# Chunk-wise start and half-wise end of layer 1, with its score rows and two own-row loads moved, in a four-layer graph network

## The chip, the cores and the metric

The kernel runs on one core of a Trainium2 chip. The metric is the device time of one execution in microseconds. Below, PE is the tensor engine (PEld its weight loads), DVE the vector engine, ACT the scalar engine, POOL the GpSimd engine and SP the sync engine, which here only issues transfers.

## The reference

Four graph layers on 2708 nodes with 512 features; after each, the input is added and the rows are normalised. The adjacency matrix `adj` is 2708 x 2708 with about four entries per row besides the diagonal. What matters here is layer 1:

```python
type_sum_a = adj_a @ x
type_sum_b = adj_b @ x
attn_a = sigmoid(concatenate([type_sum_a, x], axis=1) @ Wa.T + ba)
attn_b = sigmoid(concatenate([type_sum_b, x], axis=1) @ Wb.T + bb)
h = x @ W_sa
s_left = h @ a_sa[0, :Hd]
s_right = h @ a_sa[0, Hd:]
scores = s_left[:, None] + s_right[None, :]
e = where(adj_a != 0, exp(-leaky_relu(scores, 0.01)), 0.0)
attn = e / (sum(e, axis=1, keepdims=True) + 1e-05)
x_a = attn @ h
x_b = adj_b @ (x @ W_gcnb) + b_gcnb
return sigmoid(attn_a * x_a + attn_b * x_b)
```

`adj_a` and `adj_b` are both `adj`. Layer 0 is `x - (adj @ x) * (diag + 1)` times a weight plus a bias, layer 2 a normalised neighbour sum, layer 3 a graph convolution with tanh.

## The kernel before, in words

The kernel finds the nonzero entries of `adj` in layer 0 and then works on lists of edges. Rows are taken in NB = 24 blocks of R = 113 rows. The edges of a block, some 450, stand in a list of 512 places, that is EC = 4 chunks of 128. To sum a block's neighbours, POOL gathers the source rows of the four chunks from a table in HBM (`gather`, L602: four indirect DMAs, one per chunk, with one row of the table per partition; places without an edge are skipped), and PE multiplies each chunk by a 128 x 113 matrix that holds each edge's value in the column of its target row. [...]

The order of work is written out by hand (`manual_schedule`), so each engine executes its instructions in the order of the program, and waits in that order.

Layer 0 leaves `table[0]` in HBM, one row of 1029 float32 per node: a one, `h`, `x @ W_gcnb`, then the node's `s_right` and gate terms. It leaves the node's `s_left` in a column of `xr`. The last store to the table is that of window 21 (`store0(KB - 1)`, L1297), and the gathers of layer 1 wait for it. Behind that store, SP loads own rows.

Own rows are a block's own 113 rows of `table[0]`, needed for the diagonal. They lie in NO = 9 places inside buffers that layer 0 has done with (`own_place`, L643). Blocks 0 to 3 are loaded by SP at L1278, 4 to 6 at L1295, 7 and 8 at L1299 (`load_own1`; each is two DMAs, of 112 rows and of 1). From block 9 on, POOL gathers them with one indirect DMA each (`gather_own1`, L1394), in step i for block i + 8, once the place is free.

Layer 1 itself (from L1634): `s_left` is needed as a row on all partitions. `spread_left(i)` (L1377) has PE transpose four blocks' columns into PSUM and DVE copy them out (L1383). Six such calls stand before the loop. The loop has one step per block i:

- `gather1(i + 2)`: POOL's four issues into one of three buffers `gath`, after PE has done with the block that used it.
- `sums1(i)`: PE sums the rows weighted with the edge values, `l1s`, L1441, 8 matmuls in 16 passes.
- `both1(i - 1)`: DVE joins the two sums of the block before: `rec`, `l1a` (L1492), `l1v` (L1497), then ACT's tanh.
- `values1(i + 2)`: ACT makes the value matrices `s`, in two parts.
- `scored_sums1(i)`: PE sums with the scores, `l1e`, L1451, 16 passes. Its PSUM tile exists once, so it waits for `l1a` of block i - 1.
- `scores1(i + 1)`: DVE adds and applies the leaky slope (L1424, L1428; the tile `e`), ACT the exponential; `mask1` (L1434) clears places without an edge.
- `stats1(i - 1)`, `gates1(i)`, `gated1(i)` (`l1b`, L1471 and L1475), then `mask1(i + 1)`, `scale1`, `norm1(i - 2)` with its store to `table[1]`, and `source_sum(i)`.

After the loop come `both1(23)`, `stats1(23)` and `norm1(23)`, the last store to `table[1]`, and then the gathers of layer 2, which wait for it. Before the loop DVE also works out `in_block` and `block_of` (L1338, L1344), used by `source_sum`, and `plus` (L1590). `keep_warm` and `keep_busy` are matmuls into tiles that nobody reads.

Of the kernel before, what the change touches and what calls it, by code (L numbers as in the profile page):

```python
# [18 lines left out]
R = 113  # L19
# [428 lines left out]
def sparse_stack(  # L448
# [148 lines left out]
    def over_chunks(row):  # L597
        return row[:, None, :].to_broadcast([P, EC, R])
# [63 lines left out]
    with ExitStack() as phase:  # L662
# [632 lines left out]
                    load_own1(i)  # L1295
        keep_busy(4)
        store0(KB - 1)  # L1297
        for i in range(7, NO):
            load_own1(i)  # L1299


    gpool = ctx.enter_context(tc.tile_pool(name="gpool", bufs=1))
# [26 lines left out]
    for k, t in enumerate((ba_bc, bb_bc)):  # L1329
# [4 lines left out]
    nc.vector.reciprocal(inverse, inverse)  # L1334


    in_block = gpool.tile([P, NB, NS], I32, name="in_block")
    nc.vector.tensor_scalar(  # L1338
        in_block, where_all, 1.0 / R, 0.5 / R - 0.5, op0=ALU.mult, op1=ALU.add
    )  # L1340
    block_of = gpool.tile([P, NB, NS], FP, name="block_of")
    for g, (c0, _) in enumerate(SEGS):
        at = slice(8 * g, 8 * g + 8)
        nc.vector.tensor_scalar(  # L1344
            block_of[:, :, at], in_block[:, :, at], float(c0), None, op0=ALU.add
        )
    deg_k = gpool.tile([P, KB], FP, name="deg_k")

    def source_sum(b):
# [14 lines left out]
    def halves(t, r):  # L1364
        return t[:r, :].rearrange("p (k d) -> p k d", k=2)
# [11 lines left out]
    def spread_left(i, n=4):  # L1377
        ps = ps_sp.tile([P, n, P], FP, tag="sp", name=f"sl{i}")
        for k in range(n):
            nc.tensor.transpose(  # L1380
                ps[:, k, :R], cols[:R, i + k, 0:1].to_broadcast([R, P]), ident[:R, :R]
            )
        nc.vector.tensor_copy(s_left[:, i : i + n, :], ps[:, :, :R])  # L1383
# [21 lines left out]
    def gather1(i):  # L1405
        gather(gath[i % NGB], i, table[0], W1)

    def values1(i, chunks):

        if i not in edge_s:  # L1410
            edge_s[i] = spool.tile([P, EC, R], FP, tag="s", name=f"s1_{i}", bufs=3)
            nc.scalar.copy(gath[i % NGB][:, :, W1], inverse[:, i, :])
        for c in chunks:
            t = spool.tile([P, R], FP, tag="away", name=f"away1_{i}_{c}")
            nc.scalar.activation(t, iota_r, AF.Abs, bias=nrow[:, i, c : c + 1])
            nc.scalar.activation(  # L1416
                edge_s[i][:, c, :], t, AF.Relu,
                bias=edges[:, i, c, 1:2], scale=nvalue[:, i, c : c + 1],
            )

    def scores1(i):

        e = spool.tile([P, EC, R], FP, tag="e", name=f"e{i}")
        nc.vector.tensor_tensor(  # L1424
            e, gath[i % NGB][:, :, SR : SR + 1].to_broadcast([P, EC, R]),
            over_chunks(s_left[:, i, :]), ALU.add,
        )
        nc.vector.scalar_tensor_tensor(e, e, 0.01, e, op0=ALU.mult, op1=ALU.max)  # L1428
        nc.scalar.activation(e, e, AF.Exp, scale=-1.0)
        edge_e[i] = e  # L1430

    def mask1(i):
        e = edge_e[i]
        nc.vector.scalar_tensor_tensor(e, edge_s[i], 0.0, e, op0=ALU.is_gt, op1=ALU.mult)  # L1434

    def sums1(i):
        g, s, r = gath[i % NGB], edge_s.pop(i), rows(i)
        sum_s[i] = ps_1s.tile([P, 2, D], FP, tag="s1", name=f"l1s{i}")
        for k, at in enumerate(s_at):
            for c in range(EC):  # L1440
                nc.tensor.matmul(  # L1441
                    sum_s[i][:r, k, : at.stop - at.start], lhsT=s[:, c, :r], rhs=g[:, c, at],
                    start=(c == 0), stop=(c == EC - 1),
                )

    def scored_sums1(i):
        g, e, r = gath[i % NGB], edge_e.pop(i), rows(i)
        sum_e[i] = ps_1e.tile([P, 2, D], FP, tag="e1", name=f"l1e{i}")
        for k, at in enumerate(e_at):
            for c in range(EC):  # L1450
                nc.tensor.matmul(  # L1451
                    sum_e[i][:r, k, k : k + at.stop - at.start], lhsT=e[:, c, :r],
                    rhs=g[:, c, at], start=(c == 0), stop=(c == EC - 1),
                )

    def gates1(i):

# [21 lines left out]
        )  # L1479
        nc.scalar.activation(vb[:r, :], vb[:r, :], AF.Copy, scale=gate[:r, 1:2])  # L1480

    def both1(i):

        r, agg = rows(i), sum_e.pop(i)
        rec = small.tile([P, 1], FP, tag="rec", name=f"rec{i}")
        nc.vector.scalar_tensor_tensor(
            rec[:r, :], agg[:r, 0, 0:1], 1e-5, ediag[:r, i : i + 1], op0=ALU.add, op1=ALU.add
        )
        nc.vector.reciprocal(rec[:r, :], rec[:r, :])
        nc.vector.tensor_mul(rec[:r, :], rec[:r, :], gate1.pop(i)[:r, 0:1])  # L1490
        va = work.tile([P, D], FP, tag="u", name=f"l1a{i}")
        nc.vector.scalar_tensor_tensor(  # L1492
            halves(va, r), halves(own1.pop(i)[:, 1 : D + 1], r), ediag[:r, i : i + 1],
            agg[:r, :, 1 : H + 1], op0=ALU.mult, op1=ALU.add,
        )
        v = work.tile([P, D], FP, tag="v", name=f"l1v{i}")
        nc.vector.scalar_tensor_tensor(  # L1497
            v[:r, :], va[:r, :], rec[:r, :], vb1.pop(i)[:r, :], op0=ALU.mult, op1=ALU.add
        )

        nc.scalar.activation(v[:r, :], v[:r, :], AF.Tanh, scale=0.5)
        v1[i] = v

    def stats1(i):
        r, v = rows(i), v1[i]
        nc.vector.scalar_tensor_tensor(
            v[:r, :], v[:r, :], 0.5, xr[:r, i, :], op0=ALU.mult, op1=ALU.add
        )
        stats = small.tile([P, 6], FP, tag="stats", name=f"st_l1_{i}")
        nc.vector.bn_stats(stats[:r, :], v[:r, :])  # L1510
        k = i % 2
        if k == 0 or i >= NB - 2:
            mv2[0] = small.tile([P, 2, 4], FP, tag="mv4", name=f"mv_l1_{i}")
        mv = mv2[0]
        nc.vector.bn_aggr(mv[:r, k, 0:2], stats[:r, :])
        v1[i] = v, mv[:, k, :]
        if k == 0 and i < NB - 2:
            return

        at = slice(k, k + 1) if i >= NB - 2 else slice(0, 2)  # L1520
        n = at.stop - at.start
        nc.vector.tensor_scalar(mv[:r, at, 1], mv[:r, at, 1], 1e-5, None, op0=ALU.add)
        nc.gpsimd.tensor_tensor(
            mv[:r, at, 2], mv[:r, at, 1], root[:r, :].to_broadcast([r, n]), ALU.pow
        )
        unscaled[0] = r, mv, at
# [60 lines left out]

    plus = const.tile([P, NB], FP, name="plus")
    inv_norm = const.tile([P, NB], FP, name="inv_norm")
    nc.vector.tensor_scalar(plus, adiag, 0.0, None, op0=ALU.is_gt)  # L1590

    def row_norms(at, on_pool=True):
        n = at.stop - at.start
# [40 lines left out]
    gather1(0)  # L1634
    values1(0, range(EC))
    gather1(1)
    values1(1, range(EC))
    for i in range(0, NB, 4):
        spread_left(i)
    spread_bias(bg_bc)  # L1640
    scores1(0)
    mask1(0)
    for i in range(NB):
        if i + 2 < NB:
            gather1(i + 2)
# [24 lines left out]
        if i > 1:  # L1670
            norm1(i - 2)
        if i + 1 == NB:
            norm1(i - 1)
        if i + 1 == NB:
            nc.sync.dma_start(out=b3_bc[0:1, :], in_=b3[None, :])
            nc.sync.dma_start(out=w3_sb, in_=w3T.rearrange("(b p) o -> p b o", p=P))
        if i < KB:
            source_sum(i)
        if i == KB:
            source_sums_out()  # L1680
            row_norms(slice(0, KB))
    copy_norm(0)
    copy_norm(1)
    keep_warm(ps_sp, "sp", [P, 4, P], 8)
    both1(NB - 1)
    spread_row(b3_bc, "b3")
    stats1(NB - 1)
    scale1()
    norm1(NB - 1)
    deg_ps = source_sums_in()  # L1690
# [234 lines left out]
```

## Time and profile before

| | us |
|---|---|
| time, median of 3 runs | 973.66 |
| lowest and highest run | 972.88, 977.18 |
| the profiled execution's own time | 958.69 |
| its span | 956.9 |
| PE / DVE / ACT / POOL busy in it | 884.8 / 685.3 / 526.3 / 465.5 |

Layer 1's first gather is issued at 414.26 us of the span, its loop runs to about 607, and layer 2's first gather is issued at 618.51. The profiled execution is one execution; stretches of it are compared with stretches of it, and a difference found so is carried over to the median. Matmul records show a modelled end, so PE's busy time says less than its waits. Rows of POOL's indirect DMAs show the time of issuing, not of the transfer.

### The profile page before, as it was taken

What the parts mean: (1) busy time and instruction counts of PE and PEld (TensorE: products, weight loads), DVE (VectorE), ACT (ScalarE), POOL (GpSimd) and SP (SyncE); (2) the same over time, 40 slices, a digit from 0 to 9 for tenths busy, and PEclk for the clock granted to TensorE, in tenths of its full rate; (3) what the DMA queues carried; (4) which work ended last, traced back from release to release, by engine and by line L of the source; (5) the groups of instructions that cost most, each with busy time, mean ns of one, the idle gap of its engine ahead of it and who ended that gap; (6) DMA issues with size and microseconds to landing.
All of it is one profiled execution on the core that took longest, in us unless ns stands there. A gap on an engine that the chain in (4) does not pass through costs nothing.

```text
span 956.9 us, 11163 instructions
## 1 busy us (share of the span) xinstructions
PE 884.8 (92%) x2957; PEld 489.4 (51%) x2957; DVE 685.3 (72%) x1811; ACT 526.3 (55%) x1221; POOL 465.5 (49%) x518
## 2 busy tenths in 40 slices
PE   6889999999999999989999999798888899999993
PEld 2446565556565565557777777433233334444441
DVE  7788798888888853148999999777777436565553
ACT  5776676867677672347777777344544312222221
POOL 3323131432323230057777753377777477766630
PEclk7879999999999999989999999989999999999997
DMA  9986887988878454388999976367777466555531
GB/s 245 323 208 184 216 229 207 272 223 220 227 206 238 152 166 126 115 286 292 349 330 342 341 276 236 95 188 213 212 218 217 131 170 189 163 174 162 151 107 32
DMA packets 133717, 201.73 MB, mean 211 GB/s; under 512 B 82658, under 2 KB 82704, under 8 KB 133647
## 3 DMA queue, kind: packets, MB, share of 16 engines
q0 software_dynamic: 39024, 118.69, 40.2%
q1 hardware_dynamic: 94623, 82.25, 30.2%
q8 instruction: 26, 0.43, 0.2%
q14 instruction: 44, 0.36, 0.1%
HBM read 182.81 MB, written 27.80 MB: 220 GB/s over the span
## 4 chain that ended last, share of the span: by engine, by line
PE 58%; DMA 14%; DVE 14%; issue 5%; ACT 4%; SPq 3%; POOL 2%; POOLq 0%; DVEq 0%; ACTq 0%
PE o_l L588 15%; DMA gath<-table,source 11%; PE l3a L617 8%; PE hb L588 7%; PE h L588 7%; PE l0a L617 6%; PE l2a L617 2%; PE fetched L929 2%; POOL gath L604 2%; PE unread L1585 2%; DVE l1b L1471 1%; SPq L691 1%; DMA gath<-in_x_dram 1%; DVE l1b L1475 1%; DVE l1a L1492 1%
## 5 line engine op out<-in xcount | busy, mean ns | idle before, releaser
L604 POOL DMA_INDIRECT gath<-table,source x288 | 305.0, 1059 | 102.7 <-issue 49.0
L604 POOL DMA_INDIRECT gath<-in_x_dram,source x96 | 97.4, 1015 | 224.9 <-issue 190.7
L617 PE MATMUL l2a<-gath,s_left 128*113 128x512 f32 (+1 forms) x192 | 97.2, 624 | 17.6 <-DMA gath<-table,source 17.4
L1451 PE MATMUL l1e<-gath,e 128*113 128x257 f32 (+3 forms) x384 | 88.4, 383 | 10.4 <-DVE l1a L1492 10.4
L617 PE MATMUL l3a<-gath,s 128*113 128x512 f32 (+1 forms) x192 | 88.3, 603 | 2.7 <-DMA gath<-table,source 2.7
L1441 PE MATMUL l1s<-gath,s 128*113 128x256 f32 (+3 forms) x384 | 89.8, 387 | 0.0
L617 PE MATMUL l0a<-gath,s 128*113 128x512 f32 (+1 forms) x192 | 87.5, 596 | 0.1
L588 PE MATMUL o_l<-shared,xi_own 128*113 128x512 f32 (+1 forms) x192 | 86.5, 593 | 0.8 <-ACT xi_own L581 0.7
L588 PE MATMUL hb<-w_gc_sb,xi_own 128*128 128x512 f32 (+1 forms) x176 | 83.3, 601 | 0.0
L1451 PEld LDWEIGHTS l1e<-gath,e 128*113 128x113 f32 (+1 forms) x384 | 66.2, 177 | 32.7 <-PE l1s L1441 19.4
L588 PE MATMUL o_l<-w_sb,uw_own 128*128 128x512 f32 (+1 forms) x176 | 82.7, 614 | 0.2
L588 PE MATMUL h<-w_sa_sb,xi_own 128*128 128x259 f32 (+1 forms) x352 | 80.8, 382 | 0.0
L1441 PEld LDWEIGHTS l1s<-gath,s 128*113 128x113 f32 (+1 forms) x384 | 69.2, 181 | 17.8 <-ACT s L1416 1.5
L588 PEld LDWEIGHTS h<-w_sa_sb,xi_own 128*128 128x128 f32 (+1 forms) x352 | 64.8, 185 | 19.8 <-issue 6.1
L617 PEld LDWEIGHTS l2a<-gath,s_left 128*113 128x113 f32 (+1 forms) x192 | 30.4, 181 | 73.9 <-DMA gath<-table,source 53.9
L1844 ACT ACTIVATE y<-l3v,mv_l 113x512 f32<-113x512 f32 (+1 forms) x24 | 19.5, 813 | 86.2 <-DVE mv_l L1840 79.2
L588 PEld LDWEIGHTS o_l<-shared,xi_own 128*113 128x113 f32 (+1 forms) x192 | 33.9, 177 | 49.2 <-issue 47.1
L617 PEld LDWEIGHTS l0a<-gath,s 128*113 128x113 f32 (+1 forms) x192 | 33.5, 179 | 40.7 <-issue 35.5
L617 PEld LDWEIGHTS l3a<-gath,s 128*113 128x113 f32 (+1 forms) x192 | 32.5, 180 | 41.2 <-issue 37.9
L1818 DVE SCALAR_TENSOR_TENSOR l3v<-o_l,d_inv,b_bc 113x512 f32<-113x512 f32 (+1 forms) x25 | 18.1, 728 | 48.1 <-PE o_l L588 48.1
L1308 DVE TENSOR_SCALAR s<-niota_r,nrow,edges 128x113 f32<-128x113 f32 x192 | 51.5, 344 | 0.0
L876 DVE FIND_INDEX8 where_all<-rec_all,shared 128x8 uint32<-128x678 f32 (+1 forms) x64 | 51.2, 800 | 0.0
(256 smaller groups left out, 1580.6 us busy)
## 6 DMA issues: line engine op xcount, KB each, us to landing
shared<-in_adj_dram SPq DMA_DIRECT2D x14, 1186.5 KB
table<-st SPq DMA_DIRECT2D x21, 514.5 KB
gath<-in_adj_dram SPq DMA_DIRECT2D x7, 1186.5 KB
gath<-in_x_dram SPq DMA_DIRECT2D x21, 256.0 KB
xi_own<-in_x_dram SPq DMA_DIRECT2D x23, 224.0 KB
table<-xr SPq DMA_DIRECT2D x23, 224.0 KB
table<-y SPq DMA_DIRECT2D x23, 224.0 KB
out_dram<-y SPq DMA_DIRECT2D x23, 224.0 KB
```

Source lines behind the costliest of these rows:

```text
L588: nc.tensor.matmul(o, lhsT=uT[:, f, :r], rhs=w[:, f, :], start=(f == 0), stop=(f == DB - 1))
L604: nc.gpsimd.indirect_dma_start(out=g[:, c, :n], out_offset=None, in_=src[:, :], in_offset=bass.IndirectOffsetOnAxis(ap=source[:, i, c : c ...
L617: nc.tensor.matmul(agg[:r, :], lhsT=s[:, c, :r], rhs=g[:, c, off : off + D], start=(c == 0), stop=(c == EC - 1),)
L691: nc.sync.dma_start(out=a[:TAIL, NF, :r], in_=adjT[NF * P :, at])
L876: nc.vector.max_index(out=where_all[:, i, g * 8 : (g + 1) * 8], in_max=top, in_values=seg)
L929: nc.tensor.matmul(t["fetched"][:, c, : 3 * NS], lhsT=t["q"][:, c * P : (c + 1) * P], rhs=rec_all[:, i].rearrange("p k s -> p (k s)"), sta ...
L1308: nc.vector.tensor_scalar(s[:, c, :], niota_r, nrow[:, i, c : c + 1], edges[:, i, c, 1:2], op0=ALU.is_equal, op1=ALU.mult,)
L1441: nc.tensor.matmul(sum_s[i][:r, k, : at.stop - at.start], lhsT=s[:, c, :r], rhs=g[:, c, at], start=(c == 0), stop=(c == EC - 1),)
L1451: nc.tensor.matmul(sum_e[i][:r, k, k : k + at.stop - at.start], lhsT=e[:, c, :r], rhs=g[:, c, at], start=(c == 0), stop=(c == EC - 1),)
L1585: nc.tensor.matmul(o[:, :cols], lhsT=ident, rhs=bg_bc[:, :cols], start=True, stop=True)
L1818: nc.vector.scalar_tensor_tensor(v[:r, at], o[:r, at], d_inv[:r, i : i + 1], b3_bc[:r, at], op0=ALU.mult, op1=ALU.add,)
L1844: nc.scalar.activation(y[:r, :], v[:r, :], AF.Identity, bias=mv[:r, 3:4], scale=mv[:r, 2:3])
```

## The change

It has four parts. The function bodies of the loop stay as they are but for these.

1. SP no longer loads the own rows of blocks 7 and 8; POOL gathers them, after the gather of block 1 and before that of block 2.
2. Block 0's scores and masks are made in two halves of two chunks, and its matmuls go through the chunks in the outer loop (both column halves of chunk 0, then chunk 1, and so on).
3. Of the six `spread_left` calls, two (blocks 0 to 7) stay before the loop, with two unread matmuls behind them on PE; the other four stand at the ends of steps 1 to 4, before `source_sum`. The work on `in_block`, `block_of` and `plus` is moved behind the bias copy.
4. The last block's `both1` and `stats1` work in two column halves of 256.

```diff
         store0(KB - 1)
-        for i in range(7, NO):
-            load_own1(i)
...
-    def scores1(i):
+    def scores1(i, at=slice(0, EC)):
-        e = spool.tile([P, EC, R], FP, tag="e", name=f"e{i}")
+        if i not in edge_e:
+            edge_e[i] = spool.tile([P, EC, R], FP, tag="e", name=f"e{i}")
+        e, n = edge_e[i][:, at, :], at.stop - at.start
...
-    def mask1(i):
-        e = edge_e[i]
-        nc.vector.scalar_tensor_tensor(e, edge_s[i], 0.0, e, op0=ALU.is_gt, op1=ALU.mult)
+    def mask1(i, at=slice(0, EC)):
+        e = edge_e[i][:, at, :]
+        nc.vector.scalar_tensor_tensor(
+            e, edge_s[i][:, at, :], 0.0, e, op0=ALU.is_gt, op1=ALU.mult
+        )
+    def in_turn(i, parts):
+        both = [(k, at, c) for k, at in enumerate(parts) for c in range(EC)]
+        return sorted(both, key=lambda t: t[2]) if i == 0 else both
     def sums1(i):
-        for k, at in enumerate(s_at):
-            for c in range(EC):
+        for k, at, c in in_turn(i, s_at):
...
     def scored_sums1(i):
-        for k, at in enumerate(e_at):
-            for c in range(EC):
+        for k, at, c in in_turn(i, e_at):
...
-    def both1(i):
+    def both1(i, parts=2):
+        for k in range(0, 2, parts):
+            kk, at = slice(k, k + parts), slice(k * H, (k + parts) * H)
+            nc.vector.scalar_tensor_tensor(
+                halves(va, r)[:, kk, :], halves(own, r)[:, kk, :], ediag[:r, i : i + 1],
+                agg[:r, kk, 1 : H + 1], op0=ALU.mult, op1=ALU.add,
+            )
+            nc.vector.scalar_tensor_tensor(
+                v[:r, at], va[:r, at], rec[:r, :], vb[:r, at], op0=ALU.mult, op1=ALU.add
+            )
+            nc.scalar.activation(v[:r, at], v[:r, at], AF.Tanh, scale=0.5)
...
-    def stats1(i):
+    def stats1(i, parts=1):
+        for k in range(parts):
+            at = slice(k * D // parts, (k + 1) * D // parts)
+            nc.vector.scalar_tensor_tensor(
+                v[:r, at], v[:r, at], 0.5, xr[:r, i, at], op0=ALU.mult, op1=ALU.add
+            )
+            nc.vector.bn_stats(stats[:r, k, :], v[:r, at])
...
     gather1(0)
     values1(0, range(EC))
     gather1(1)
+    for i in (7, 8):
+        gather_own1(i)
     values1(1, range(EC))
-    for i in range(0, NB, 4):
+    for i in (0, 4):
         spread_left(i)
+    unread = ps_1s.tile([P, 2, D], FP, tag="s1", name="unread")
+    for _ in range(2):
+        nc.tensor.matmul(
+            unread[:, 0, :], lhsT=ident[:R, :], rhs=xr[:R, 0, :], start=True, stop=True
+        )
     spread_bias(bg_bc)
+    in_block = gpool.tile([P, NB, NS], I32, name="in_block")
...
-    scores1(0)
-    mask1(0)
+    for at in (slice(0, 2), slice(2, EC)):
+        scores1(0, at)
+        mask1(0, at)
     for i in range(NB):
...
+        if 0 < i and 4 * i + 4 < NB:
+            spread_left(4 * i + 4)
         if i < KB:
             source_sum(i)
...
-    both1(NB - 1)
+    both1(NB - 1, 1)
     spread_row(b3_bc, "b3")
-    stats1(NB - 1)
+    stats1(NB - 1, 2)
```

More of the change, by code (lines that the diff above doesn't have):

```diff
@@ L1334, in sparse_stack @@
     nc.vector.reciprocal(inverse, inverse)
[L1337 to L1346, printed above, removed]
     deg_k = gpool.tile([P, KB], FP, name="deg_k")
@@ L1419, in values1 @@
             )
-    def scores1(i):
-        e = spool.tile([P, EC, R], FP, tag="e", name=f"e{i}")
+    def scores1(i, at=slice(0, EC)):
+        if i not in edge_e:
+            edge_e[i] = spool.tile([P, EC, R], FP, tag="e", name=f"e{i}")
+        e, n = edge_e[i][:, at, :], at.stop - at.start
         nc.vector.tensor_tensor(
-            e, gath[i % NGB][:, :, SR : SR + 1].to_broadcast([P, EC, R]),
-            over_chunks(s_left[:, i, :]), ALU.add,
+            e, gath[i % NGB][:, at, SR : SR + 1].to_broadcast([P, n, R]),
+            s_left[:, i, None, :].to_broadcast([P, n, R]), ALU.add,
         )
@@ L1429, in scores1 @@
         nc.scalar.activation(e, e, AF.Exp, scale=-1.0)
-        edge_e[i] = e
-    def mask1(i):
-        e = edge_e[i]
-        nc.vector.scalar_tensor_tensor(e, edge_s[i], 0.0, e, op0=ALU.is_gt, op1=ALU.mult)
+    def mask1(i, at=slice(0, EC)):
[6 more added lines that the diff above has]
+        return sorted(both, key=lambda t: t[2]) if i == 0 else both
     def sums1(i):
@@ L1438, in sums1 @@
         sum_s[i] = ps_1s.tile([P, 2, D], FP, tag="s1", name=f"l1s{i}")
-        for k, at in enumerate(s_at):
-            for c in range(EC):
[L1441 to L1444, printed above, removed]
+        for k, at, c in in_turn(i, s_at):
+            nc.tensor.matmul(
+                sum_s[i][:r, k, : at.stop - at.start], lhsT=s[:, c, :r], rhs=g[:, c, at],
+                start=(c == 0), stop=(c == EC - 1),
+            )
     def scored_sums1(i):
@@ L1448, in scored_sums1 @@
         sum_e[i] = ps_1e.tile([P, 2, D], FP, tag="e1", name=f"l1e{i}")
-        for k, at in enumerate(e_at):
-            for c in range(EC):
[L1451 to L1454, printed above, removed]
+        for k, at, c in in_turn(i, e_at):
+            nc.tensor.matmul(
+                sum_e[i][:r, k, k : k + at.stop - at.start], lhsT=e[:, c, :r],
+                rhs=g[:, c, at], start=(c == 0), stop=(c == EC - 1),
+            )
     def gates1(i):
@@ L1491, in both1 @@
         va = work.tile([P, D], FP, tag="u", name=f"l1a{i}")
[L1492 to L1495, printed above, removed]
         v = work.tile([P, D], FP, tag="v", name=f"l1v{i}")
[L1497 to L1501, printed above, removed]
+        own, vb = own1.pop(i)[:, 1 : D + 1], vb1.pop(i)
+        for k in range(0, 2, parts):
[8 more added lines that the diff above has]
+            nc.scalar.activation(v[:r, at], v[:r, at], AF.Tanh, scale=0.5)
         v1[i] = v
-    def stats1(i):
+    def stats1(i, parts=1):
         r, v = rows(i), v1[i]
[L1506 to L1510, printed above, removed]
+        stats = small.tile([P, 2, 6], FP, tag="stats", name=f"st_l1_{i}")
+        for k in range(parts):
+            at = slice(k * D // parts, (k + 1) * D // parts)
+            nc.vector.scalar_tensor_tensor(
+                v[:r, at], v[:r, at], 0.5, xr[:r, i, at], op0=ALU.mult, op1=ALU.add
+            )
+            nc.vector.bn_stats(stats[:r, k, :], v[:r, at])
         k = i % 2
@@ L1514, in stats1 @@
         mv = mv2[0]
-        nc.vector.bn_aggr(mv[:r, k, 0:2], stats[:r, :])
+        nc.vector.bn_aggr(mv[:r, k, 0:2], stats[:r, :parts, :])
         v1[i] = v, mv[:, k, :]
@@ L1589, in sparse_stack @@
     inv_norm = const.tile([P, NB], FP, name="inv_norm")
-    nc.vector.tensor_scalar(plus, adiag, 0.0, None, op0=ALU.is_gt)
     def row_norms(at, on_pool=True):
@@ L1636, in sparse_stack @@
     gather1(1)
+    for i in (7, 8):
+        gather_own1(i)
     values1(1, range(EC))
-    for i in range(0, NB, 4):
+    for i in (0, 4):
         spread_left(i)
-    spread_bias(bg_bc)
-    scores1(0)
-    mask1(0)
+    unread = ps_1s.tile([P, 2, D], FP, tag="s1", name="unread")
+    for _ in range(2):
+        nc.tensor.matmul(
+            unread[:, 0, :], lhsT=ident[:R, :], rhs=xr[:R, 0, :], start=True, stop=True
+        )
+    spread_bias(bg_bc)
+    in_block = gpool.tile([P, NB, NS], I32, name="in_block")
+    nc.vector.tensor_scalar(
+        in_block, where_all, 1.0 / R, 0.5 / R - 0.5, op0=ALU.mult, op1=ALU.add
+    )
+    block_of = gpool.tile([P, NB, NS], FP, name="block_of")
+    for g, (c0, _) in enumerate(SEGS):
+        at = slice(8 * g, 8 * g + 8)
+        nc.vector.tensor_scalar(
+            block_of[:, :, at], in_block[:, :, at], float(c0), None, op0=ALU.add
+        )
+    nc.vector.tensor_scalar(plus, adiag, 0.0, None, op0=ALU.is_gt)
+    for at in (slice(0, 2), slice(2, EC)):
+        scores1(0, at)
+        mask1(0, at)
     for i in range(NB):
```

## Prediction

> **What bounds the kernel now.** I read the page's totals, then its 40 slices, then the chain of waits and the timelines of the stretch that the change touches: 384 to 445 us (the end of layer 0 and the first steps of layer 1) and 595 to 620 us (the last block of layer 1). Three views carry the argument.
>
> First, the busy time by stretch. The columns after the span are PE, PEld, DVE, ACT, POOL, the granted clock, the DMA share and GB/s.
>
> ```profile
> 415.00:422.00 7.00, 4.83 (x18) 2.43 (x18) 4.72 (x14) 6.05 (x17) 5.22 (x6) 0.83 0.92 283
> 422.00:428.00 6.00, 6.00 (x19) 4.52 (x19) 2.58 (x4) 2.20 (x6) 4.74 (x5) 0.63 0.95 353
> 440.00:500.00 60.00, 56.41 (x254) 43.91 (x253) 54.78 (x144) 45.85 (x117) 46.84 (x45) 1.00 0.93 325
> ```
>
> From 422 to 428 DVE is idle more than half the time while the DMA engines are 95% busy: the start of layer 1 waits for gathers. From 440 to 500 DVE has 54.8 of 60 us, with only short gaps: the loop is DVE's. That PE has 56.4 does not contradict this, as the waits of 440 to 606 show who waits for whom:
>
> ```profile
> PEld l1e L1451 <- PE l1s L1441: 18.9, 22, 1.1
> PE l1e L1451 <- DVE l1a L1492: 10.2, 22, 0.7
> ```
>
> All 22 times PE stands 0.3 to 0.6 us before `l1e(i)` for DVE's `l1a(i-1)`, and no line of that view has DVE waiting for a gather. A step takes 7.47 and 7.78 us in turn (`l1e` at 442.52, 450.30, 457.77).
>
> Second, the chain of waits at the seam, in order of time (start, us, what):
>
> ```profile
> 423.34 5.89 DMA gath<-table,source
> ...
> 429.35 0.64 DVE e L1424
> ...
> 434.25 0.67 DVE l1a L1492
> ```
>
> The last chunk of block 1's gather is issued at 423.34 and lands at 429.23; DVE's scores `e(1)` follow at once, and 5.6 us of DVE work later `l1a(0)` frees PE's `l1e(1)` at 435.06. Block 0 (`l1e(0)` from 427.54) isn't on this chain.
>
> Third, POOL, which issues every gather:
>
> ```profile
> 428.70 0.99 POOL L604 DMA_INDIRECT gath<-table,source  x1 [0.30 <-issue]
> 430.36 1.15 POOL L604 DMA_INDIRECT gath<-table,source  x1 [0.66 <-PE l1e L1451]
> ...
> 439.19 1.00 POOL L604 DMA_INDIRECT gath<-table,source  x1 [2.01 <-PE l1e L1451]
> ```
>
> An issue costs 0.99 + 0.30 = 1.29 us. POOL is issuing without pause from 414.26 to 430 and again from 439 to about 549 (46.8 busy + 45 gaps of 0.30 = 60.3 of 60 us); its only slack in between is 0.36 + 1.7.
>
> [...] own-row loads and gathers together hold 0.92 of the engines from 415 to 422. [...] Here 0.99 us is shown and the landing comes a median of 5.9 us after issue. [...] halves cost more than half; the last block of layer 3 shows it (a 256-wide half takes 0.44, a whole 0.74). [...] The trace has 0.63 of the clock in 422 to 428.
>
> **The change part by part.**
>
> *Own rows of blocks 7 and 8.* Four SP issues behind the last `table<-st` store go; two POOL gathers come, between those of blocks 1 and 2. The 0.94 MB moved by SP's queue in 412 to 436 was 13.9% of 24 us, so 3.3 us of all 16 engines, most of it ahead of the first gather, in time that is otherwise idle. Gain: blocks 0 and 1 can land earlier. Bounds: nothing (POOL's issues at 414.26 to 423.34 don't move, as they wait for the same store) and 2.4 us (landing 3.5 after issue, an estimate: layer 2's emptier queue has 3.9 at 628.35 to 632.27). I take 1.0, since gathers alone also run the engines at 0.95. Cost: all four issues of block 2 move by 2 x 1.29 = 2.6 us, its last from 428.70 to 431.3. It lands at 431.3 + 3.9 = 435.2 at best, 431.3 + 5.9 = 437.2 if the queue stays as full; the bytes ahead of it grow by those of two own gathers. I take 436.3. In the kernel before, DVE took `e(2)` up at 435.69. With `e(1)` 1.0 earlier it would be ready at 434.7, so it now waits for block 2: **+0.6** (-0.5 to +1.5). Here the whole early start is lost. Queued behind that wait on DVE are `stats1(0)`, the gates, `mask1(2)` and `both1(1)`, and PE's `l1e(2)` waits for the last. POOL's later work is caught up by its slack of about 2.1: block 4's gather keeps its 439.2, to within a microsecond.
>
> *First block by chunks.* The first half of the scores starts when chunk 1 has landed (about 420 to 421), not chunk 3 (DVE at 424.33). Its exponential stands on ACT behind block 1's values, which end at 421.3; so masks at about 422.2 and 423.8, `l1s(0)` by chunk until about 422.6, and `l1e(0)` near 422.6, 5 us before 427.54. This costs three more DVE and one more ACT instruction in time that DVE had idle. It is worth **0** by itself: the next DVE work, `e(1)`, waits for block 1 whatever block 0 does. Two warming matmuls (4 passes of 0.43, 1.7 us) lie in PE's idle 414.4 to 416.9: 0.
>
> *s_left at the ends of steps 1 to 4.* Four of six copies leave 417.57 to 420.6, where DVE was ahead of the gathers: gain 0. They come back in the loop, between `mask1`/`scale1` and `source_sum`, so ahead of `both1(i)`, for which PE's `l1e(i+1)` waits.
>
> ```profile
> 420.00 0.63 DVE L1383 COPY s_left<-sl 128x452 f32<-128x452 f32 x1 [0.31 <-PE sl L1380]
> ```
>
> 0.63 + 0.02 gap = 0.65 each, four times: **+2.6** (0 if they fell into waits; but the loop's one DVE wait, 0.3 for ACT's `row_cnt`, lies earlier in the step). Their four transposes take 0.94 / 8 = 0.12 each, 0.5 a step on PE after `l1e(i)`; PE's wait of 0.3 to 0.6 grows by the copy's 0.65 and covers them: 0. If that cover went, 0.5 a step. The moved block numbers (`in_block`, `block_of`) and `plus`, 1.5 us, lie in DVE's wait for chunk 1.
>
> *Last block by halves.* Before, from `l1a` at 609.30 to the end of the statistics at 613.03: 3.73, with 0.70 of it DVE waiting for the tanh. After: eight halves of 0.44 and gaps, 3.7, the tanh covered. **0** (-0.4 to +0.3). Whatever this is goes on to layer 2, whose first gather waits for this block's store (618.51).
>
> **Sum.** 0.6 + 2.6 + 0 = +3.2 us: span 956.9 to 960.1, own time 958.69 to 961.9. The profiled execution lies 15.0 below the median of the runs, 973.66; I carry the difference over: **976.9**, a change of 0.33%.
>
> **Rivals.** *(a) The early start is kept.* If the gathers land as fast as the engines can, `e(1)` comes 2.4 earlier, block 2 is not late, and copies are paid: -2.4 + 2.6 = +0.2, 973.9. If the copies are hidden as well, 971.3; the full 5 us of `l1e(0)` would give 968.7. For it: the 3.3 us of transfers removed. Against: POOL's unbroken issue row and the 0.95.
> *(b) PE's clock makes it clearly slower.* With block 0 done early, PE stands idle for some 3 us before `l1e(1)` at about 434. The trace before has half clock after such a gap, for 6.8 us (passes of 0.43 for 0.215). If it lasts one such stretch, `l1e(1)`, the transposes and `l1s(2)` end at about 444.4, 0.6 late; [...] until `l1s(2)` ends, +4.9, 981.8. It decides from a low stretch of over 7 us at 433. For it: 0.63 in the view above. [...]
> *(c) The change doesn't do what it says:* the landings stay at POOL's pace of 1.29 a chunk, so "as they land" moves nothing, and block 2 comes with the full 5.9: +1.5 + 2.6 = +4.1, 977.8.
>
> **How the numbers follow.** A measurement of this kernel can tell about 0.5%, 4.9 us. Forecast with its bounds (+1.5 to +4.1, so (c) too): 0.65; (a) 0.20; (b) 0.15. Slower by over 0.5% is (b) at its longer stretches (0.12) and the upper end of the forecast with the runs' own spread, 972.88 to 977.18 (0.13): 0.25. Faster by that much is only (a)'s last case: 0.07. The rest, 0.68, is within. The range leaves out the ends of (a) and (b): 971.0 to 980.6.
>
> **What would show it.** Right: `l1e(0)` near 422.6, `e(1)` at about 428.3 but `e(2)` waiting for a gather until about 436; steps 1 to 4 longer by 0.65 and later ones unchanged at 7.47 and 7.78; `l1e(5)` about 3.2 after 465.54; the last block's 3.73 unchanged. Wrong: `e(2)` taken up before 435 or without a wait; steps 1 to 4 of the old length; a clock under 1.00 after 430; DVE waiting for gathers past step 5.

## The result, and the profile after

Both kernels were run 20 times. The median of the changed kernel is 979.1 us (970.2 to 985.3), that of the kernel before 976.1 us (971.9 to 983.1). The ratio is 1.0018 with a 95% interval of 0.9999 to 1.0038, so +1.8 us (-0.1 to +3.7): less than this measurement can tell from no change. It is not the quotient of the two medians, which would be 1.0031 (+3.0 us), and here and below it leaves out runs in a slow state (here the one of 985.3 us). The forecast was +3.2 us, and 976.9 us as a time.

One thing must be known to read the numbers below. Each group of runs had a kernel before of its own beside it, and its median lay either at 958 to 959 us or at 976 to 977 us. The profile of before belongs to the **lower level** (own time 958.69). The three runs in its table, the runs of the result, and the profile of the changed kernel that came with them (span 975.5) belong to the **upper level**. The change is therefore read in a second profile of the changed kernel, taken at the lower level (run e12_after_third, span 959.4), and ratios are always taken within a group.

A place of 400 us or more, in the text as in the lines of profiles, is us of the profile's own span. A smaller one is us after the issue of layer 1's first gather (at 414.26 in the span before, 410.87 and 412.07 in the two spans after). It serves to compare profiles, since they enter layer 1 up to 5 us apart, and are already 4 us apart at layer 0's first `hb` matmul, near 80 us, in code that is the same in all.

The busy time by stretch of the changed kernel (upper level), at the same distance from the first gather as the first two rows shown of before (the third is the loop, 440 to 500 in both); columns as there:

```profile
411.61:418.61 7.00, 4.48 (x12) 1.97 (x11) 4.21 (x12) 6.39 (x18) 5.22 (x6) 0.86 0.79 241
418.61:424.61 6.00, 5.83 (x16) 3.92 (x16) 1.61 (x5) 2.40 (x7) 4.73 (x5) 0.60 0.97 351
440.00:500.00 60.00, 56.58 (x264) 44.66 (x263) 53.95 (x141) 42.74 (x107) 46.44 (x42) 1.00 0.91 318
```

DVE has even less to do in the second row (1.61 of 6 us, before 2.58): the start still waits for gathers, and POOL's column is what it was (5.22 and 4.73, before 5.22 and 4.74). The chain of waits at the seam, of the changed kernel at the lower level (start, us, what):

```profile
412.07 1.01 POOL gath L604
...
423.73 0.99 POOL xi_own L1384
...
429.32 5.27 DMA gath<-table,source
...
434.72 0.64 DVE e L1414
...
440.00 0.54 DVE s_left L1371
```

Before, the chain ran through block 1's last chunk (423.34, landing 5.9 later) and `e(1)`. Now it runs along POOL's issues, through an own gather (L1384), to block 2's last chunk at 429.32 and to `e(2)` at 434.72. The timeline of POOL, same kernel, shows what stands between blocks 1 and 2:

```profile
421.14 0.99 POOL L604 DMA_INDIRECT gath<-table,source  x1 [0.30 <-issue]
422.44 0.99 POOL L1384 DMA_INDIRECT xi_own<-table,own_at  x1 [0.30 <-issue]
423.73 0.99 POOL L1384 DMA_INDIRECT xi_own<-table,own_at  x1 [0.30 <-issue]
425.03 0.99 POOL L604 DMA_INDIRECT gath<-table,source  x1 [0.30 <-issue]
```

Two issues of 1.29 us. The timeline of DVE, same kernel, with the wait before each row in brackets:

```profile
426.87 0.63 DVE L1414 TENSOR_TENSOR e<-gath,s_left 128x452 f32<-128x452 f32 x1 [3.54 <-DMA gath<-table,source]
...
434.72 0.63 DVE L1414 TENSOR_TENSOR e<-gath,s_left 128x452 f32<-128x452 f32 x1 [1.43 <-DMA gath<-table,source]
...
439.92 0.62 DVE L1371 COPY s_left<-sl 128x452 f32<-128x452 f32 x1
440.46 0.35 DVE L1340 SCALAR_TENSOR_TENSOR in_block<-block_of,rec_all 128x192 int32<-128x192 f32 x1
```

`e(2)` now waits 1.43 us for block 2, where it waited for nothing before. The moved copy follows DVE's `mask1` without a gap, and the next instruction starts 0.54 us after it. The timeline of DVE before has two of the copies in 1.16 us together, the mask and the next instruction 0.54 us apart, and `e(2)` without a wait:

```profile
416.20 1.16 DVE L1383 COPY s_left<-sl 128x452 f32<-128x452 f32 x2
...
432.89 0.62 DVE L1434 SCALAR_TENSOR_TENSOR e<-s,e 128x452 f32<-128x452 f32 x1
433.43 0.35 DVE L1352 SCALAR_TENSOR_TENSOR in_block<-block_of,rec_all 128x192 int32<-128x192 f32 x1
...
435.69 0.63 DVE L1424 TENSOR_TENSOR e<-gath,s_left 128x452 f32<-128x452 f32 x1
```

Last, the timeline of PE, changed kernel at the lower level:

```profile
424.11 3.63 PE L1445 MATMUL l1e<-gath,e 128*113 128x257 f32 x16
...
432.57 3.69 PE L1445 MATMUL l1e<-gath,e 128*113 128x257 f32 x16 [1.34 <-DVE l1a L1490]
...
442.08 3.69 PE L1445 MATMUL l1e<-gath,e 128*113 128x257 f32 x16 [1.95 <-DVE l1a L1490]
```

`l1e(1)` and `l1e(2)` still stand behind DVE's `l1a`. The wait behind the late gather and the copy, 1.95, is longer than any of before's (0.7 at most in its first profile, 1.13 in its second, run e9). After step 4 the steps are 7.48 and 7.76 us, as before. `l1e(5)`, for which the forecast was 3.2 us later, starts 54.68 us after the first gather (before 51.29 and, in e9, 51.88), so 3.4 or 2.8 later.

### The profile page after: what moved, and what is told of

The parts are those of the page before. It is cut to its first block, busy times and chain, and to the rows that moved or that the text cites. A ratio compares the mean times of both kernels' runs of the same rounds, so it can differ in the third digit from the quotient of the medians.

```text
span 975.5 us, 11156 instructions
## 1 busy us (share of the span) xinstructions
PE 886.4 (91%) x2961; PEld 493.6 (51%) x2961; DVE 685.7 (70%) x1818; ACT 525.8 (54%) x1223; POOL 469.8 (48%) x520
## 4 chain that ended last, share of the span: by engine, by line
PE 64%; DVE 15%; DMA 5%; ACT 4%; issue 4%; another core or an unknown queue 3%; SPq 2%; POOL 1%; POOLq 0%; DVEq 0%; ACTq 0%
PE o_l L588 15%; PE l3a L617 8%; PE l2a L617 8%; PE hb L588 7%; PE h L588 7%; PE l0a L617 6%; PE unread L1584 3%; PE l1e L1445 2%; PE fetched L929 2%; DMA gath<-table,source 2%; DVE l1b L1465 1%; DVE l1b L1469 1%; SPq L691 1%; DVE l1a L1490 1%
## 5 line engine op out<-in xcount | busy, mean ns | idle before, releaser
L1445 PE MATMUL l1e<-gath,e 128*113 128x256 f32 (+3 forms) x384 | 90.9, 391 | 14.9 <-DVE l1a L1490 8.5
L617 PE MATMUL l2a<-gath,s_left 128*113 128x512 f32 (+1 forms) x192 | 93.8, 628 | 3.8 <-DMA gath<-table,source 2.7
L1436 PE MATMUL l1s<-gath,s 128*113 128x261 f32 (+3 forms) x384 | 90.7, 389 | 2.7 <-DMA gath<-table,source 2.5
L1445 PEld LDWEIGHTS l1e<-gath,e 128*113 128x113 f32 (+1 forms) x384 | 68.2, 182 | 37.6 <-issue 11.6
L588 PE MATMUL o_l<-w_sb,uw_own 128*128 128x512 f32 (+1 forms) x176 | 80.6, 601 | 0.2
L1584 PE MATMUL unread<-bg_bc,ident 128*128 128x512 f32 x80 | 42.7, 649 | 24.0 <-remote 19.4
L617 PEld LDWEIGHTS l2a<-gath,s_left 128*113 128x113 f32 (+1 forms) x192 | 33.8, 189 | 54.4 <-issue 41.9
```

Of the source, the lines that this page charges most:

```text
L588: nc.tensor.matmul(o, lhsT=uT[:, f, :r], rhs=w[:, f, :], start=(f == 0), stop=(f == DB - 1))
L617: nc.tensor.matmul(agg[:r, :], lhsT=s[:, c, :r], rhs=g[:, c, off : off + D], start=(c == 0), stop=(c == EC - 1),)
L1436: nc.tensor.matmul(sum_s[i][:r, k, : at.stop - at.start], lhsT=s[:, c, :r], rhs=g[:, c, at], start=(c == 0), stop=(c == EC - 1),)
L1445: nc.tensor.matmul(sum_e[i][:r, k, k : k + at.stop - at.start], lhsT=e[:, c, :r], rhs=g[:, c, at], start=(c == 0), stop=(c == EC - 1),)
L1584: nc.tensor.matmul(o[:, :cols], lhsT=ident, rhs=bg_bc[:, :cols], start=True, stop=True)
```

## The experiments

The kernels ran in three groups, e1 to e4, e5 to e8 and e9 to e12, with before at 958.7, 977.2 and 958.2 us. The table gives for each kernel the ratio to before in its own group with its interval, and where four DVE instructions start in its one profile. The two profiles of before show how far such places scatter without any change: by 0.6 us for `e(1)` and 1.5 us for `l1a(23)`, as two steps of e9 happen to wait 0.26 and 0.43 us for a gather. So the length of single steps says more than the last column. The moved block numbers and `plus` and the two unread matmuls are in no kernel but the changed one, e10 and e11; no run tests them alone.

| kernel | ratio (95%) | `e(1)` | `e(2)` | `l1a(1)` | `l1a(23)` |
|---|---|---|---|---|---|
| lower level | | | | | |
| before, first profile | 1 | 15.10 | 21.44 | 27.37 | 195.04 |
| before, second profile (e9) | 1 | 15.69 | 22.04 | 27.97 | 196.51 |
| e1: copies only | 1.0033 (1.0018 to 1.0049) | 15.62 | 22.02 | 28.49 | 198.00 |
| e2: own gathers only | 1.0021 (1.0006 to 1.0035) | 15.49 | 22.79 | 28.75 | 196.42 |
| e3: chunks only | 0.9984 (0.9967 to 1.0001) | 15.11 | 21.47 | 27.40 | 195.37 |
| e4: halves only | 0.9993 (0.9982 to 1.0004) | 15.29 | 21.64 | 27.57 | 195.19 |
| e10: changed, own rows by SP | 1.0017 (1.0005 to 1.0029) | 14.70 | 21.04 | 27.52 | 196.83 |
| e11: changed, own gathers later | 1.0041 (1.0024 to 1.0058) | 14.44 | 20.78 | 27.25 | 197.23 |
| e12: changed | 1.0045 (1.0027 to 1.0063) | 14.79 | 22.65 | 29.12 | 198.46 |
| upper level | | | | | |
| changed, with the result | 1.0018 (0.9999 to 1.0038) | 15.58 | 24.86 | 32.28 | 202.50 |
| e8: changed | 1.0025 (1.0008 to 1.0041) | 14.54 | 22.27 | 30.42 | 200.58 |
| e7: chunks and halves only | 1.0000 (0.9979 to 1.0020) | 15.32 | 21.99 | 27.98 | 197.23 |
| e5: 23 copies | 1.0093 (1.0067 to 1.0118) | 15.39 | 22.60 | 29.06 | 208.06 |
| e6: five own gathers | 1.0077 (1.0048 to 1.0106) | 14.65 | 29.01 | 34.96 | 205.38 |

**e1, the copies alone.**

```diff
-    for i in range(0, NB, 4):
+    for i in (0, 4):
         spread_left(i)
...
+        if 0 < i and 4 * i + 4 < NB:
+            spread_left(4 * i + 4)
         if i < KB:
             source_sum(i)
```

> The kernel before with the third part alone: four of the six spreads of s_left moved to the ends of steps 1 to 4. Theory of the prediction (the loop is DVE's, a copy ahead of both1 costs its length): steps 1 to 4 longer by 0.65 us each, later steps unchanged, +2.6 us (ratio 1.0027). Rival (the copies fall into waits of DVE): steps 1 to 4 of the old length, 0 us (1.000). Rival (removing four copies from the start lets the first block begin earlier): e(1) earlier, ratio below 1.000.

The length of a step is the distance between two `l1a`. The timeline of DVE, e1, step 1:

```profile
432.80 0.74 DVE L1492 SCALAR_TENSOR_TENSOR l1a<-shared,ediag,l1e 113x512 f32<-113x512 f32 x1
...
439.53 0.62 DVE L1383 COPY s_left<-sl 128x452 f32<-128x452 f32 x1
440.06 0.35 DVE L1352 SCALAR_TENSOR_TENSOR in_block<-block_of,rec_all 128x192 int32<-128x192 f32 x1
...
440.80 0.74 DVE L1492 SCALAR_TENSOR_TENSOR l1a<-shared,ediag,l1e 113x512 f32<-113x512 f32 x1
```

Steps 1 to 4 take 8.00, 8.34, 7.99 and 8.34 us (before 7.46, 7.78, 7.48, 7.77): +2.18 in all, 0.54 each. The fifth step is 7.48. The time says +3.2 us (1.7 to 4.7). The copies are paid, by 0.54 instead of 0.65; they fall into no wait.

**e2, the own gathers alone.**

```diff
-        for i in range(7, NO):
-            load_own1(i)
...
     gather1(1)
+    for i in (7, 8):
+        gather_own1(i)
     values1(1, range(EC))
```

> The kernel before with the first part alone: own rows of blocks 7 and 8 gathered by GpSimd between blocks 1 and 2. Theory of the prediction: e(1) up to 1 us earlier relative to the first gather's issue, block 2's four issues 2.6 us later, DVE waits for block 2's gather before e(2), net +0.6 us (-0.5 to +1.5; ratio 1.0005). Rival (the start is gained, block 2 not late): e(1) 2.4 us earlier, no wait before e(2), -2.4 us (0.9975). Rival (the landing keeps its full 5.9 us): e(2) waits 1.5 us, 1.0015.

Block 1's last chunk lands at 15.37 (before 14.97 and 15.56), block 2's at 22.67 (20.46 and 20.03), `e(2)` waits 0.86 us for it and starts at 22.79:

```profile
437.06 0.63 DVE L1422 TENSOR_TENSOR e<-gath,s_left 128x452 f32<-128x452 f32 x1 [0.86 <-DMA gath<-table,source]
```

Step 1 is 8.43 instead of 7.46, +0.97. The time says +2.0 us (0.6 to 3.4). Nothing is gained at the start. Block 2 is late, and costs more than the 0.6 of the theory and less than the 1.5 of the last rival.

**e3, the chunks alone**: `scores1`, `mask1`, `in_turn` and the two sums as in the diff of the change, everything else as before.

> The kernel before with the second part alone: block 0's scores and masks in two halves, its matmuls chunk by chunk; all six spreads stay ahead. Theory of the prediction: l1e(0) begins up to 5 us earlier, e(1) does not, as it waits for block 1: 0 us (1.000). Rival (PE's idle time before l1e(1) brings a stretch at half clock): l1e(1) takes over 5 us instead of 3.7, +1 to +5 us (1.001 to 1.005). Rival (the start is kept): e(1) and l1e(1) earlier, -2 us or more (0.998).

All four places are those of before's first profile to 0.1 us, apart from the last (195.37). `l1e(0)` starts at 13.65, no earlier than before (13.50 and 13.58): PE has the transposes and the bias until 8.6, and then `l1s(0)`, for the most part at half clock (5.20 us for its 16 rows, which take 3.65 in the loop at a clock of 1.00), until 13.6. So the chunks bring nothing here; the time, -1.5 us (-3.2 to +0.1), cannot be told from nothing either.

**e4, the halves alone**: `both1(NB - 1, 1)` and `stats1(NB - 1, 2)` with their bodies.

> The kernel before with the fourth part alone: the last block's both1 and stats1 in two halves. Theory of the prediction: from l1a(23) to the end of the statistics 3.7 us as before (3.73), 0 us (1.000; -0.4 to +0.3). Rival (the halves let the tanh run beside DVE and win its 0.7 us): 3.0 us, 0.9993. Rival [...]: 4.3 us, 1.0006.

The timeline of DVE, e4, last block (the first `l1a`, the first and last row of the statistics):

```profile
609.83 0.47 DVE L1496 SCALAR_TENSOR_TENSOR l1a<-w_sb,ediag,l1e 109x256 f32<-109x256 f32 x1
...
611.73 0.42 DVE L1512 SCALAR_TENSOR_TENSOR l1v<-l1v,xr 109x256 f32<-109x256 f32 x1
...
612.97 0.43 DVE L1515 BATCH_NORM_STATS2 st_l<-l1v 109x6 f32<-109x256 f32 x1
```

The same of before:

```profile
609.30 0.74 DVE L1492 SCALAR_TENSOR_TENSOR l1a<-w_sb,ediag,l1e 109x512 f32<-109x512 f32 x1
...
611.60 0.69 DVE L1506 SCALAR_TENSOR_TENSOR l1v<-l1v,xr 109x512 f32<-109x512 f32 x1 [0.70 <-ACT l1v L1501]
612.33 0.69 DVE L1510 BATCH_NORM_STATS2 st_l<-l1v 109x6 f32<-109x512 f32 x1
```

From 609.83 to 613.40 are 3.57 us (before, from 609.30, 3.73). The wait of 0.70 for the tanh is gone; as only about 0.16 is won, the halves cost some 0.54 more than wholes. The time, -0.7 us (-1.7 to +0.4), agrees and settles nothing.

**e5, the copy 23 times.** All six spreads stay ahead, and one more is made at the end of every step up to 22.

```diff
+        if i + 1 < NB:
+            spread_left(4 * (i % 6))
         if i < KB:
             source_sum(i)
```

> The kernel before with all six spreads ahead of the loop kept, and one spread of s_left made once more (four transposes, one copy, the same values into the same place) at the end of every step from 0 to 22. Theory (a copy at that place costs a step what the first four did, 0.51 to 0.57 us, since DVE's instruction ahead of both1 waits for nothing else): 23 x 0.54 = +12.4 us, ratio 1.013. Rival (the 0.5 was of the seam, the loop itself hides a copy): under +3 us, 1.003. Rival (full price 0.65 and the transposes too): +15 us or more, 1.016.

Up to step 18 every step is 7.99 or 8.3 us long. From `l1a(0)` to `l1a(23)`, between which 22 of the 23 copies lie, it takes 187.0 us. That is 11.9 more than before's first profile (175.1), and 22 x 0.54 = 11.9; it is 11.0 more than before's second (176.0), and 10.2 more than e7 at e5's own level (176.8), some of whose steps have a short wait of DVE for PE (0.33 in the one at 494 us of its span). The time says +9.1 (6.5 to 11.5), under the 12.4 expected; where the rest went is not shown. A copy at that place costs a step about 0.5 us all along the loop.

**e6, five own gathers.**

```diff
-                for i in range(4, 7):
-                    load_own1(i)
-        for i in range(7, NO):
-            load_own1(i)
...
     gather1(1)
+    for i in range(4, NO):
+        gather_own1(i)
```

> The kernel before with the own rows of blocks 4 to 8, not only 7 and 8, gathered by GpSimd between the gathers of blocks 1 and 2. Theory (each such gather delays block 2's issues by 1.29 us, and e(2) waits for block 2): e(2) later by 1.35 us (what two gathers gave) + 3 x 1.29 = 5.2 us than before, part of it caught up in later steps or not at all; e(1) unmoved at 15.1 to 15.6 us after the first gather's issue, since POOL's pace sets it; ratio 1.003 to 1.006. Rival (SP's transfers held the first landings back): e(1) 1 us or more earlier than 15.1. Rival (POOL's slack and the engines' own limit hide the three more): e(2) no later than with two gathers, 1.002.

`e(2)` comes at 29.01, 7.0 after e7's, but not for a gather: DVE had stood before `gate(0)`, for PE. The price per gather can't be read from it; what it shows instead is in the last section. That `e(1)` comes 0.7 before e7's with five SP loads fewer is less than the 1 us of the rival, and no second run tests it.

**e7, chunks and halves only.** The edits of e3 and e4 together.

> The kernel before with the second and fourth part only: first block by chunks, last block by halves; own rows by SP and all spreads ahead of the loop as before. Theory (parts add up): 0.9984 x 0.9993 = 0.9977, the loop's steps unchanged at 7.47 and 7.78, the tail 3.57. Rival (the first one's 0.9984 was the spread of executions and not the chunks, whose e(1) did not move): 0.9993.

1.0000: the two parts that cost nothing bring nothing that can be measured. The 0.9984 of e3 did not come back. No kernel tried is shown to beat the one before.

**e8, the changed kernel again (upper level).**

> The changed kernel once more, for a second profile beside these. Theory (the halt of 2.9 us of DVE, POOL and PE at 431 to 433.7 and the stretch at half clock behind it belong to that one execution): l1a(0) at about 20.4 us after the first gather's issue instead of 23.3, l1e(1) in 3.7 us at full clock, steps 1 to 4 of 8.0 to 8.9 us, ratio about 1.003 as the parts add up. Rival (the half clock belongs to the change): l1e(1) again takes over 5 us, and the halt or a wait of PE over 3 us stands before it.

`l1a(0)` is at 20.74, as expected, but the halt comes back: DVE waits 1.29 us before `rec(0)`, and `l1e(1)` takes 5.37 us (3.69 at full clock) in a stretch of half clock of 3.4 us. So the halt is not one execution's. Whether it is the change's, the third group asks.

**e9, the kernel before again.**

> The kernel before, unchanged, for a profile of it beside those below. Theory (PE's semaphore updates that reach other engines late belong to the place of execution, where the kernel before too takes about 977 and not 958 us): if this group of runs has before at about 977, its profile shows DVE and PE in layer 2 waiting for updates that no recorded instruction explains, and fewer recorded updates (670, not 1006, of semaphore 100), but l1a(0) at 20 to 21 us after the first gather's issue; if it has before at about 958, none of them. Rival (they belong to the kernels tried): none here, whatever the time.

It came at the lower level (959.23) and shows no such wait, and 1006 updates of semaphore 100. There is no profile of before at the upper level. That the halts of layer 2 come with this level and not with the change rests on e5 and e7, which do not have the changed kernel's seam and show them.

**e10, own rows by SP again.** The reverse of e2's edit, on the changed kernel.

> The changed kernel with its first part undone: own rows of blocks 7 and 8 loaded by SP again. Theory (the parts add up; GpSimd's two gathers cost 1.3 us where PE's updates are prompt and some 3 to 5 us more where they come late at the seam): steps 1 to 4 at 8.0 and 8.34, step 1 without the wait for block 2, ratio 1.001 (1.0033 x 0.9984 x 0.9993), 1 to 3 us under the changed kernel. Rival (the wait sits in the chunks or the copies): l1a(1) still 8.4 to 9.7 us behind l1a(0).

Step 1 is 8.00, where the changed kernel has 9.52, and `e(2)` waits for nothing:

```profile
431.67 0.62 DVE L1416 TENSOR_TENSOR e<-gath,s_left 128x452 f32<-128x452 f32 x1
```

`l1a(23)` is 1.63 earlier than the changed kernel's, the ratio 1.0017 against 1.0045 (the intervals overlap by a hair). Block 1's last chunk lands at 14.57, with SP's loads in the way again (14.67 without them in e12): they did not hold it back.

**e11, own gathers in steps 4 and 5.**

```diff
-    for i in (7, 8):
-        gather_own1(i)
...
         if i + 2 < NB:
             gather1(i + 2)
+        if i in (4, 5):
+            gather_own1(i + 3)
```

> The changed kernel with the two own gathers issued by GpSimd in steps 4 and 5, behind those of blocks 6 and 7, instead of before block 2. Theory (their place, not their issuer, delays block 2): e(2) without a wait, l1a(1) 8.0 behind l1a(0), steps 4 to 6 at most 0.3 us longer as GpSimd then issues 6 transfers of 1.29 = 7.7 us in a step of 7.5 to 8.3; ratio 1.001, as with SP. Rival (GpSimd has no room in the loop): steps 5 to 8 longer by 1 us in all or more, 1.002.

`e(2)` waits for nothing, as the theory says, and steps 4 to 7 keep their length. But POOL has no slack from step 4 to step 8 (in e10 it has 1.6 us in step 4 and 0.4 each in steps 6 and 8), and step 8 is 8.45 instead of 7.75, as the timeline of DVE shows:

```profile
490.19 0.63 DVE L1414 TENSOR_TENSOR e<-gath,s_left 128x452 f32<-128x452 f32 x1 [0.60 <-DMA gath<-table,source]
```

Block 9's last chunk is issued 1.3 us later than in e10 and lands 6.25 us after its issue (6.55 there), so the issue is late and not the transfer; in e9's two waits it was the transfer (7.5 us). That is 0.7 lost of 1.5 won in step 1; from `l1a(0)` to `l1a(23)` e11 takes 178.0 us, the changed kernel 178.8, e10 177.3. The time (1.0041, 1.0024 to 1.0058) does not confirm the gain: its interval holds the changed kernel's own 1.0045. Whether the later place is worth anything stays open.

**e12, the changed kernel at the lower level.**

> The changed kernel itself beside them. Theory: if before is at about 958 here, no halt at the seam, l1a(1) 9.0 us (8.43 + 0.55) behind l1a(0), steps 2 to 4 at 8.34, 7.99 and 8.34, ratio 1.003 (1.0033 x 1.0021 x 0.9984 x 0.9993); if at about 977, the halt of 1 to 3 us before rec(0) again, ratio 1.002 to 1.003. Rival (the halt belongs to the change and not to the place of execution): the halt also at 958.

No halt: DVE goes from `source_sum(0)` straight to `rec(0)`, and PE's clock is full from 424.1 to the last block (1.00 in 440 to 500, and every `l1e` and `l1s` takes 3.63 to 3.69 us). Step 1 is 9.52, steps 2 to 4 are 8.34, 7.99 and 8.35. The time is +4.3 us (2.6 to 6.0); the product of the four parts is 1.0031, inside the interval. Its profile was shown above.

## Why the prediction was right, point by point

The forecast of +3.2 us lies inside the +1.8 (-0.1 to +3.7) of the result and between it and the +4.3 (2.6 to 6.0) of the lower level. The result alone does not confirm it, as its interval holds 0 too; the steps of e1, e2, e10 and e12 do. Its two costly terms are the two that cost. Their sizes were off in opposite directions, the own rows' by 0.4 to 1.0 too small and the copies' by 0.4 too large, so that the sum fits as well as it does is partly luck.

- **Own rows, +0.6 forecast.** That block 2 is late and the whole early start is lost is what happened: `e(2)` comes at 22.8 without an earlier start (e2) and at 22.65 with one (e12). The landing was taken as 22.04 after the first gather (436.3 in the span before) and is 22.52 and 22.67, since it follows the issue by 5.3 to 5.4, where 5.0 was assumed (before 6.0 and 5.6; the 3.9 of its best case never came). That is nearly rival (c)'s case; the term is 1.0 by e2's step 1, and 1.5 by step 1 of e10 against e12 (1.6 by `l1a(23)`). The gain of 1.0 assumed from SP's 3.3 us of transfers is none: from chunk to chunk block 1 lands one POOL issue (about 1.28 us) apart with and without them. Nor did they run for the most part ahead of the first gather: of the 0.94 MB, 0.48 moved before 414.3 us of the span before, and 0.46 from there to 418. `e(1)` is indeed about 0.7 earlier in the three kernels e10 to e12 than in the six others of that level, but in e10 with SP's loads. These three are also the only ones of that level with the moved block numbers and the unread matmuls; what brings it was not isolated. POOL's slack was judged rightly: block 4's first gather comes at 25.74 (before 24.93 and 25.54).
- **Copies, +2.6 forecast.** 2.18 or 2.19 in e1, e10 and e11, and about 0.54 a step in e5 and e12 too. What was mis-sized is 0.63 + 0.02 = 0.65: the duration of the row instead of its distance to the next start. The traces have 0.54 from the start of a copy or a mask to the next start, for a row of 0.62 to 0.63, so the two rows overlap. The kernel before already had it, in the mask (432.89 to 433.43) and in the first two of these very copies, two rows of 0.62 that take 1.16 us together. The row that the forecast shows (420.00) has a wait on either side, so its distance to a next start says nothing of an unbroken row. The transposes are hidden, as forecast: they take 0.55 us, and PE still waits 0.44 to 0.78 before `l1e` in steps 3 to 5 of e12.
- **Chunks, 0 forecast.** Right in what they are worth, wrong in the place: `l1e(0)` starts at 12.0 and not 8.3, because `l1s(0)` needs all four chunks, the last of which lands at 9.5, and runs at half clock until 12.0 (5.44 us for its last 12 rows, where the loop has 3.65 for 16). In the kernel before, too, the last chunk had landed only at 9.85 (424.11), so the 422.6 contradicted its own trace; it carried no term.
- **Halves, 0 forecast (-0.4 to +0.3).** About -0.16 by the trace of e4, in one profile.
- **Rival (b), the clock.** Not at the lower level: PE waits 1.34 before `l1e(1)`, not 3, and no slow stretch follows (`l1e(1)` in 3.69 us). At the upper level it happens in the changed kernel (last section): the clock under 1.00 after 430, named as a sign of being wrong, is in the profile that came with the result (0.50 from 433.66 to 440.49). Still the ratio there is not higher. How long a gap must be to halve the clock is not shown: before, the clock halves at 419.60, 2.7 us after the end of PE's longest wait since 414 us, which was 2.45. And in its sums "+4.9, 981.8" is 4.9 on top of the 3.2.
- **Rival (a)** is out: nothing of the start is kept past `e(2)`, and block 2 is late.
- **The carry-over.** "The profiled execution lies 15.0 below the median; I carry the difference over" joined two levels. It did no harm, since the difference lies elsewhere: from layer 2's first gather to the end the nine profiles of the lower level take 337.6 to 340.2 us, the five of the upper 351.4 to 356.4.

## What to carry to other kernels

Price a DVE instruction that stands among others without waits by the distance between starts (here 0.54), not by its duration (0.62 to 0.63), and check it by repeating it in every step. Where one engine issues all gathers at a fixed pace (here one in about 1.29 us), look at which block's last chunk is waited on *after* the edit: two extra issues ahead of block 2 took back all that an earlier block 0 and 1 could give. When a profile and the times differ by more than their spread, find out first in which stretch, before anything is carried from one to the other.

## What the runs showed of the hardware

**Two levels of time.** The upper level was not expected. Its five profiles have waits whose release no recorded instruction explains ("remote"), mostly in layer 2: the page's group line of the changed kernel reads

```profile
L1584 PE MATMUL unread<-bg_bc,ident 128*128 128x512 f32 x80 | 42.7, 649 | 24.0 <-remote 19.4
```

and in the profiles of the lower level neither PE nor DVE has one over 1 us from layer 1 on. At the seam PE's semaphore updates, by their recorded times, come late and in bursts. In e12 the four of `l1e(0)` come 0.87 us apart (425.15, 426.02, 426.89, 427.75), each with its matmul. In the changed kernel of the result the rows of `l1e(0)` end at 427.2, but the next updates of the same semaphore are recorded at 428.69, 433.65 and 433.71, and DVE's `rec(0)`, which reads `l1e(0)`, starts at 433.73. Its timelines of DVE and of PE:

```profile
433.73 0.16 DVE L1480 SCALAR_TENSOR_TENSOR rec<-l1e,ediag 113x1 f32<-113x1 f32 x1 [2.82 <-remote]
```

```profile
435.09 6.35 PE L1445 MATMUL l1e<-gath,e 128*113 128x257 f32 x16 [4.44 <-remote]
```

DVE stands for 2.82 us, PE for 4.44, and `l1e(1)` then takes 6.35 us instead of 3.7, in 6.83 us at half clock (433.66 to 440.49) that begin 3.0 us into PE's wait. So half clock came with a wait of 4.44 here, and none came after one of 1.34 (e12). At the start of layer 1 it comes with less: before, PE's rows fill 2.51 of the 3.41 us ahead of the half clock (416.19 to 419.60); in e12 it comes after no wait of PE over 0.9 us, and in e4 it does not come after one of 2.34. So no length of wait is given here as the one that halves the clock. Between 412 and 940 us, before has four half-clock stretches of 3.41 or 6.83 us, and the changed kernel of the result nine of 3.41, 6.83 or 10.24 us: one, two or three times 3.41.

In e6 the halt is longest, timeline of DVE:

```profile
437.48 0.16 DVE L1457 TENSOR_TENSOR gate<-l1s,gates 113x2 f32<-113x2 f32 x1 [8.31 <-remote]
```

`gate(0)` reads `l1s(0)`, whose last row ends at 426.4; the update is recorded at 437.46. Also, a third of the updates is missing in these profiles (676 of semaphore 100 in that of the result, 1006 before). The ends of PE's rows are modelled by the profile, so they can't tell whether the matmuls or the updates were late. What makes the level was not found. The record gives another chip for each group of experiments (5 and 14 for the two at the lower level, 0 for the one at the upper), so the chip is the nearest suspect; no chip was used in two groups, and nothing here separates the chip from the time of the runs. Between `e(1)` and `l1e(1)` the halts were seen only with own gathers ahead of block 2 (three profiles of three at that level, none of the two without), and yet the changed kernel's ratio is not higher there than at the lower level, so no cost of them is claimed.
